# A recurrent block on one core: zero matmuls at the start, the identity on ScalarE's queue, halves in the first normalisation, another order of work

## The chip, the core and the metric

The kernel runs on one core of one Trainium2 chip. The core has five queues of work: TensorE (PE: matmuls, with the loads of their stationary operands listed apart as PEld), VectorE (DVE), ScalarE (ACT), GpSimd (POOL) and SyncE (SP, which here only issues DMAs). The metric is the device time of one execution in microseconds (us), the median over the runs. All arithmetic is in 32-bit floats.

## The reference

Eight sequences of 256 rows and 512 channels go through one block: a token-shifted mix of inputs, a recurrence over time for 32 heads of 16 channels, and a gated feed-forward part. Cut to what matters:

```python
xn = _ln(x, ln1_w, ln1_b)
sx = _token_shift(xn, state[:, i1])                 # previous row minus this row
xxx = tanh((xn + sx * maa_x) @ maa_w1)              # 5 groups of 32
xxx = matmul(xxx, maa_w2)
x5 = xn[:, :, None] + sx[:, :, None] * (maa_stack + xxx)
w = exp(-exp(time_decay + tanh(x5[:, :, 1] @ decay_w1) @ decay_w2))
r, k, v = x5[3] @ Wr.T, x5[0] @ Wk.T, x5[2] @ Wv.T
g = silu(x5[4] @ Wg.T)
def step(s, rkvw):                                  # 256 steps, per head a 16 x 16 state
    a = k_t[:, :, :, None] * v_t[:, :, None, :]
    out = einsum('bhk,bhkd->bhd', r_t, u * a + s)
    return (a + w_t[:, :, :, None] * s, out)
att = group_norm(outs) * gn_w + gn_b
x = x + att * g @ Wo.T
xn2 = _ln(x, ln2_w, ln2_b); sx2 = _token_shift(xn2, state[:, i0])
rr = sigmoid((xn2 + sx2 * ffn_maa_r) @ ffn_Wr.T)
kk = square(relu((xn2 + sx2 * ffn_maa_k) @ ffn_Wk.T))
x = x + rr * (kk @ ffn_Wv.T)
```

## The kernel before

The work of one sequence (a batch, b from 0 to 7) is cut into three stages, each written by one function: `inputs_of_scan` (first normalisation, mixing, the projections to k, v, r, g and the decay w), `scan` (the recurrence) and `rest` (group norm, output projection, second normalisation, feed-forward). In one phase the kernel works on the first stage of one batch, the second of the batch before and the third of the one before that.

Rows lie on partitions only for the normalisation; then PE turns them (`turned`, the transposes against the identity `idt`), and from there on channels lie on the 128 partitions, in four blocks, two to a tile ("q" counts the two halves of the channels). PE's results go to eight banks: six tiles `ps` of one bank each and the tile `wrep`, which holds the decays of a scan. ScalarE and VectorE read them out.

The recurrence runs on VectorE as a scan along time. For each block of 128 channels of k there are four scans of 1024 elements (`st<-wrep,vs`, line 885). Before each, v is written to memory (`vo`), read back repeated over partitions (`vs<-vo`, a DMA of 512 KB), its first column is filled by ScalarE (line 876) and it is multiplied by k (line 883, on DVE, or line 880 on POOL). After it, POOL multiplies by r (line 888), and PE sums over the state's rows with a matmul against a constant, which is called the gather here (line 896).

No scheduler of the language orders the work. The stage functions only add pieces of work (`plan.add`, with an engine, an estimated length, the buffers written and read) to a `Plan`. Its table `TURNS` holds one rank for each of the 2,643 pieces. `order` takes the ready piece of lowest rank, gives it a start from the estimates, takes its buffers from the pools, and finally sorts all pieces by start: that is the order in which each engine's queue is filled. The estimates are `LATENCY` (what passes from the end of a piece on one engine until another engine may use its result), `LANDS` (the same for DMAs), `SWITCH`, `AHEAD` and `GAP`. They only decide the order and which buffer a piece gets; on the chip every engine runs its queue in order and waits on semaphores.

The start concerns the prediction most. For batch 0 the normalisation is written differently (`alone`): VectorE takes the statistics of the two halves of the rows (lines 554 and 555), ScalarE the square root of both (line 557), VectorE the reciprocal (559) and the two scaled copies xh (562). PE turns them (588). With `first` given, the input of the first mixing matmul is built from xn times (1 - maa_x), to which the shifted rows times maa_x are added (622): before the change VectorE reads `ps` to make xn (595), and ScalarE reads the same `ps` to make the product (598), for which `owners` folds the norm's weights into the table `ow`. Then come the mixing matmul (401, with weights `mw`), a tanh on ScalarE (680), a matmul against `mw2a`, and the mixed inputs (703 to 720).

`mul` (line 396) writes all larger matmuls, with the stationary operand as one piece of 128 columns or as four of 32 that run beside each other, as the plan's `tiles` decides. In the profile one matmul of 32-bit floats is two records, a transpose is one.

Of the kernel before, what the change touches and what calls it, by code (L numbers as in the profile page):

```python
# [67 lines left out]
class Plan:  # L68
# [4 lines left out]
    LATENCY = {"PE": 0.12, "DVE": 0.09, "ACT": 0.09, "POOL": 0.09, "DMA": 1.65}  # L73
    LANDS = {"vs__": (2.3, 1.8), "rsb_": (0.9, 2.0), "sq_": (0.9, 2.0), "s": (0.2, 1.9), "vo_": (0.75, 2.2), "vo__": (0.38, 2.2), "o_": (0.75, 1.1), "x": (1.6, 1.7), "xt": (1.6, 1.7), "xs": (0.7, 0.9), "rd": (0.4, 1.4)}
# [40 lines left out]
    def stage(self):  # L115
# [225 lines left out]
def tile_rwkv_block(  # L341
# [73 lines left out]
    dw1, dw2 = const("dw1", [P, NK, DEC]), const("dw2", [2 * DEC, E])  # L415
    hm = const("hm", [P, NK, 32])
    eh = const("eh", [P, 4])
    ow = const("ow", [P, 2, NK])
    W = {n: [const(f"W{n}{h}", [P, 2, E]) for h in range(2)] for n in "kvrg"}

    pool("s0", 2, [P, NK, S])
# [50 lines left out]
    def load(buf, src, kb):  # L472
        dma(buf, lambda: src, buf, kb)
# [641 lines left out]
```

## Time and profile before

| | |
|---|---|
| median of 3 runs | 616.62 us (616.23 to 616.91) |
| the profiled execution | 616.02 us |
| its span, first to last instruction | 614.2 us |
| PE busy | 593.8 us (97%) |
| VectorE busy | 546.0 us (89%) |
| POOL busy | 522.3 us (85%) |
| ScalarE busy | 515.8 us (84%) |
| DMA | 124.73 MB, mean 203 GB/s |

All times in the views count from the start of the span. A row of the timeline gives start, length, engine, line, operation, output and inputs by the program's names, the tile's shape and how many instructions are merged, and in brackets the idle time before them and what ended it. A row of the busy time by stage gives the stretch, its length, the busy time of PE, weight loads, VectorE, ScalarE and POOL, the granted clock, the share of the DMA engines and GB/s. A row of the waits gives the total, the number and the longest.

### The profile page before, as it was taken

Reading aid. Unit: us, or ns where it says so; the run is one execution under the profiler, and the core shown is the slowest. Engines: PE = TensorE matmul, PEld = TensorE weight load, DVE = VectorE, ACT = ScalarE, POOL = GpSimd, SP = SyncE. Lnnn points to the kernel's source line nnn. Section 1 sums busy time; section 2 is a strip of 40 time slices with the busy share of each in tenths; the row PEclk is TensorE's granted clock in tenths of the full one; section 3 lists DMA queues with packets and bytes.
Section 4 is the critical chain, followed back from the end, with each engine's and each line's share of the span. In section 5 each row is a group of like instructions: output and inputs, shape, how many; then the busy total and the mean of one; then the engine's idle time right before and its main releaser. Section 6 shows DMA issues by size and latency. Waiting matters only on the chain.

```text
span 614.2 us, 17191 instructions
## 1 busy us (share of the span) xinstructions
PE 593.8 (97%) x7068; PEld 345.9 (56%) x7068; DVE 546.0 (89%) x487; ACT 515.8 (84%) x1171; POOL 522.3 (85%) x421
## 2 busy tenths in 40 slices
PE   4899999899999999999999999999999999999997
PEld 4575656457544764357653885465644474456463
DVE  5789999999999989799898999999999999995432
ACT  4878878999999989999999798999899799966431
POOL 2799999999989999899978999999969998897030
PEclk9999999999999999999999999999999999999999
DMA  8887779568969777867777896796958698681551
GB/s 291 272 199 184 194 186 257 141 176 211 273 174 255 188 187 211 212 201 208 221 188 221 269 230 181 179 273 166 246 142 221 174 257 233 203 238 36 195 186 46
DMA packets 52493, 124.73 MB, mean 203 GB/s; under 512 B 5824, under 2 KB 11200, under 8 KB 52416
## 3 DMA queue, kind: packets, MB, share of 16 engines
q1 hardware_dynamic: 48048, 119.46, 71.2%
q10 hardware_dynamic: 4368, 4.20, 2.2%
q8 instruction: 55, 0.90, 0.7%
q14 instruction: 22, 0.18, 0.1%
HBM read 115.25 MB, written 8.39 MB: 201 GB/s over the span
## 4 chain that ended last, share of the span: by engine, by line
PE 73%; ACT 13%; POOL 5%; DVE 4%; issue 2%; DMA 1%; ACTq 0%; SPq 0%; POOLq 0%; DVEq 0%
PE ps L401 61%; PE ps L896 8%; PE ps L588 2%; ACT att L846 1%; PE ps L760 1%; POOL st L888 1%; ACT wrep L866 1%; POOL mix L720 1%; ACT sq L951 1%; ACT rk L951 1%; DVE st L885 1%; DMA idt<-in_consts 1%; ACT vs L876 1%; ACT att L957 1%; ACT L866 1%
## 5 line engine op out<-in xcount | busy, mean ns | idle before, releaser
L885 DVE TENSOR_TENSOR_SCAN st<-wrep,vs 128x1024 f32<-128x1024 f32 x128 | 289.5, 2280 | 4.1 <-ACT wrep L866 1.0
L888 POOL TENSOR_TENSOR st<-st,r 128x1024 f32<-128x1024 f32 x128 | 254.4, 2001 | 6.2 <-DVE st L885 5.7
L883 DVE TENSOR_TENSOR vs<-vs,ps 128x1024 f32<-128x1024 f32 x122 | 144.2, 1207 | 2.4 <-ACT vs L876 2.1
L401 PE MATMUL ps<-Ws,mix 128*32 128x512 f32 (+1 forms) x864 | 115.0, 589 | 0.8 <-ACT o L986 0.8
L401 PEld LDWEIGHTS ps<-Ws,mix 128*32 128x32 f32 (+1 forms) x864 | 37.4, 116 | 64.8 <-issue 56.9
L720 POOL TENSOR_TENSOR mix<-mix,xn 128x512 f32<-128x512 f32 x62 | 66.7, 1090 | 7.6 <-DVE mix L705 7.6
L896 PE MATMUL ps<-st,con 128*32 128x256 f32 x1024 | 61.6, 380 | 0.9 <-POOL st L888 0.4
L401 PE MATMUL ps<-mix,Wv 128*32 128x256 f32 (+1 forms) x748 | 60.0, 380 | 0.3 <-DVE mix L717 0.3
L401 PE MATMUL ps<-mix,Wr 128*32 128x256 f32 (+1 forms) x616 | 59.2, 380 | 0.6 <-ACT vs L876 0.6
L401 PE MATMUL ps<-mix,Wk 128*32 128x256 f32 (+1 forms) x856 | 58.5, 380 | 0.5 <-DVE x L968 0.3
L401 PE MATMUL ps<-mix,Wg 128*32 128x256 f32 (+1 forms) x712 | 58.6, 379 | 0.0
L401 PE MATMUL ps<-mix,Ws 128*32 128x256 f32 (+1 forms) x688 | 58.0, 380 | 0.0
L401 PE MATMUL ps<-Ws,g 128*32 128x512 f32 (+1 forms) x416 | 56.6, 593 | 0.3 <-POOL g L962 0.2
L610 POOL TENSOR_TENSOR sx<-xn 128x512 f32<-128x512 f32 x31 | 32.3, 1052 | 27.5 <-ACT xn L605 22.5
L635 POOL TENSOR_TENSOR mix<-mix,xn 128x512 f32<-128x512 f32 x44 | 47.6, 1098 | 5.0 <-ACT mix L633 3.8
L846 ACT COPY att<-ps 32x256 f32<-32x256 f32 x128 | 46.7, 365 | 4.4 <-PE ps L838 2.3
L703 ACT ACTIVATE ps<-ps,vec 128x256 f32<-128x256 f32 x112 | 46.8, 443 | 4.1 <-PE ps L401 2.7
L401 PEld LDWEIGHTS ps<-mix,Wv 128*32 128x32 f32 (+1 forms) x748 | 40.2, 120 | 16.9 <-issue 2.3
L401 PEld LDWEIGHTS ps<-mix,Wr 128*32 128x32 f32 (+1 forms) x616 | 40.6, 128 | 16.1 <-POOL mix L720 1.1
L401 PEld LDWEIGHTS ps<-mix,Ws 128*32 128x32 f32 (+1 forms) x688 | 39.9, 123 | 16.1 <-ACT mix L633 0.8
L896 PEld LDWEIGHTS ps<-st,con 128*32 128x32 f32 x1024 | 32.5, 110 | 28.0 <-POOL st L888 4.7
L401 PEld LDWEIGHTS ps<-mix,Wg 128*32 128x32 f32 (+1 forms) x712 | 39.0, 122 | 15.6 <-issue 0.3
(133 smaller groups left out, 968.0 us busy)
## 6 DMA issues: line engine op xcount, KB each, us to landing
vs<-vo SPq DMA_DIRECT2D x128, 512.0 KB, 5.5
Ws<-in_wo SPq DMA_DIRECT2D x16, 512.0 KB, 5.3
Ws<-in_fr SPq DMA_DIRECT2D x16, 512.0 KB, 6.3
Ws<-in_fk SPq DMA_DIRECT2D x16, 512.0 KB, 7.2
Ws<-in_fv SPq DMA_DIRECT2D x16, 512.0 KB, 4.9
x<-in_x SPq DMA_DIRECT2D x9, 512.0 KB, 6.5
vo<-v ACTq DMA_DIRECT2D x15, 256.0 KB, 4.6
out<-o SPq DMA_DIRECT2D x15, 256.0 KB, 4.4
```

The costliest lines, as they stand in the source:

```text
L401: nc.tensor.matmul(out[i : i + n], lhsT=w[:, i : i + n], rhs=x, start=first, stop=final)
L588: nc.tensor.transpose(ps()[:, m, n * P : (n + 1) * P], xh[n]()[:, k * P : (k + 1) * P], idt())
L610: take(512, [sx], [xn], lambda xn=xn, sx=sx, e=nc.vector if quick else nc.gpsimd: e.tensor_tensor(sx(), xn()[:, :, 0:T], xn()[:, :, 1 : T ...
L635: gp(512, t, [t, xn[q]], lambda q=q, t=t: nc.gpsimd.tensor_tensor(t(), t(), xn[q]()[:, :, 1 : T + 1], ALU.add))
L703: act(256, p_, [p_, vec], lambda g=g, q=q, m=m, p_=p_: nc.scalar.activation(p_()[:, m, :], p_()[:, m, :], AF.Identity, bias=col(f"maa_{g}" ...
L720: gp(512, t, [t, xn[q]], lambda q=q, t=t: nc.gpsimd.tensor_tensor(t(), t(), xn[q]()[:, :, 1 : T + 1], ALU.add))
L846: act(350, atts[q], [pc], lambda i=32 * (2 * q + m), m=m, q=q, h=32 * h: nc.scalar.copy(atts[q]()[h : h + 32, m, :], pc()[i : i + 32, 0, :]))
L866: act(4 * T, w, [ew], lambda m=m, w=w, ew=ew: nc.scalar.activation(w()[:, :, 1:T], ew()[:, m : m + 1, 0 : T - 1].to_broadcast([P, 4, T - 1 ...
L883: dve(4 * T, [vs], [vs, kp], lambda m=m, vs=vs, kp=kp: nc.vector.tensor_tensor(vs(), vs(), kp()[:, m : m + 1, :].to_broadcast([P, 4, T]), ...
L885: dve(4 * T, [st], [w, vs], lambda w=w, vs=vs, st=st: nc.vector.tensor_tensor_scan(st().rearrange("p n t -> p (n t)"), w().rearrange("p n ...
L888: gp(4 * T, st, [st, r], lambda m=m, st=st, r=r: nc.gpsimd.tensor_tensor(st(), st(), r()[:, m : m + 1, :].to_broadcast([P, 4, T]), ALU.mul ...
L896: nc.tensor.matmul(pat()[32 * i : 32 * i + 32, 0, :], lhsT=con()[:, s : s + 32], rhs=done[i]()[:, j, :], start=(j == 0), stop=(j == 3),)
```

## The change

Six edits:

1. `LATENCY` grows: PE from 0.12 to 0.24 us, DVE and ACT from 0.09 to 0.14, POOL from 0.09 to 0.10; `LANDS` gets an entry for `idt`. `TURNS` is replaced by another table of ranks, for 2,643 pieces of work again (the other edits add three and remove three).
2. `warmed`: seven matmuls of 128 x 256 zeros, into a `ps` tile that nothing reads; the zeros are written by a memset on VectorE at the start.
3. The identity is loaded by a DMA that ScalarE issues, instead of the fourth DMA of SP's queue.
4. For batch 0's first normalisation, each half of the rows has its own statistics, square root, reciprocal and scaled copy.
5. For batch 0, ScalarE makes the product from xn (in SBUF) instead of from `ps`.
6. `owners` becomes one instruction, 1 - maa_x.

```diff
-    LATENCY = {"PE": 0.12, "DVE": 0.09, "ACT": 0.09, "POOL": 0.09, "DMA": 1.65}
+    LATENCY = {"PE": 0.24, "DVE": 0.14, "ACT": 0.14, "POOL": 0.1, "DMA": 1.65}
...
     TURNS = """
-        5 50 8 34 35 59 43 77 41 122 129 94 125 138 20 21 22 23 145 146 152 153 18 2 26 19 38 57 32 39 58 31 33 56 44 60
...
-    ow = const("ow", [P, 2, NK])
+    ow = const("ow", [P, NK])
...
+    warm = plan.pools["xn"][3][1]
+    nc.vector.memset(warm[:, 0, :], 0.0)
...
+    def warmed():
+        ps = new("ps", "psa")
+
+        def mm():
+            for n in range(7):
+                nc.tensor.matmul(ps()[:, 0, :], lhsT=warm[:, 0, 0:P], rhs=warm[:, 0, 0:T], start=True, stop=True)
+
+        pe(5.3, [ps], [], mm)
+
     def owners():
-        i, j = (VECS.index(v) for v in ("maa_x", "ln1_w"))
-        for n in range(2):
-            gp(4, ow, [vec], lambda n=n: nc.gpsimd.tensor_tensor(
-                ow()[:, n, :], vec()[:, :, j + n], vec()[:, :, i], ALU.mult), 30)
-        for n in range(2):
-            gp(4, ow, [vec, ow], lambda n=n: nc.gpsimd.tensor_tensor(
-                ow()[:, n, :], vec()[:, :, j + n], ow()[:, n, :], ALU.subtract), 30)
+        i = VECS.index("maa_x")
+        gp(4, ow, [vec], lambda: nc.gpsimd.tensor_scalar(ow(), vec()[:, :, i], -1.0, 1.0, ALU.mult, ALU.add), 30)
...
+            if first:
+                for n in range(NT):
+                    t, s, st = new("xh", f"xh{u}_{n}"), src[n], new("st", f"st{u}_{n}")
+                    mv, rs = (mv, rs) if n == 0 else (new("mv", f"mv{u}_{n}"), new("rs", f"rs{u}_{n}"))
+                    dve(512, [st], [s], lambda st=st, s=s: nc.vector.bn_stats(out=st(), in_=s()))
+                    dve(6, [mv], [st], lambda n=n, st=st, mv=mv: nc.vector.bn_aggr(out=mv()[:, n, :], in_=st()), 8)
+                    act(1, rs, [mv, eh], lambda n=n, mv=mv, rs=rs: nc.scalar.activation(
+                        rs()[:, n : n + 1], mv()[:, n, 1:2], AF.Sqrt, bias=eh()[:, 0:1]), "sqrt", 1)
+                    dve(1, [rs], [rs], lambda n=n, rs=rs: nc.vector.reciprocal(rs()[:, n : n + 1], rs()[:, n : n + 1]), 6.25)
+                    dve(512, [t], [s, mv, rs], lambda n=n, t=t, s=s, mv=mv, rs=rs: nc.vector.tensor_scalar(
+                        t(), s(), mv()[:, n, 0:1], rs()[:, n : n + 1], ALU.subtract, ALU.mult), 0.55)
+                    xh.append(t)
+                return turned(xh, which, row, b, alone, first)
...
-                    act(256, t, [ps, ow], lambda m=m, k=k, t=t, ps=ps: nc.scalar.activation(
-                        t()[:, m, :], ps()[:, m, :], AF.Identity,
-                        bias=ow()[:, 1, k : k + 1], scale=ow()[:, 0, k : k + 1]), pointers=2)
+                    act(256, t, [xn, ow], lambda m=m, k=k, t=t, xn=xn: nc.scalar.activation(
+                        t()[:, m, :], xn()[:, m, 1 : T + 1], AF.Copy, scale=ow()[:, k : k + 1]), pointers=1)
...
-    load(idt, consts[:, 0:P], 64)
+    plan.add("ACT", 0.4, [idt], [], lambda: nc.scalar.dma_start(out=idt(), in_=consts[:, 0:P]), kb=64)
...
+    warmed()
     owners()
```

More of the change, by code (lines that the diff above doesn't have):

```diff
@@ L68 @@
 class Plan:
-    LATENCY = {"PE": 0.12, "DVE": 0.09, "ACT": 0.09, "POOL": 0.09, "DMA": 1.65}
-    LANDS = {"vs__": (2.3, 1.8), "rsb_": (0.9, 2.0), "sq_": (0.9, 2.0), "s": (0.2, 1.9), "vo_": (0.75, 2.2), "vo__": (0.38, 2.2), "o_": (0.75, 1.1), "x": (1.6, 1.7), "xt": (1.6, 1.7), "xs": (0.7, 0.9), "rd": (0.4, 1.4)}
+    LATENCY = {"PE": 0.24, "DVE": 0.14, "ACT": 0.14, "POOL": 0.1, "DMA": 1.65}
+    LANDS = {"vs__": (2.3, 1.8), "rsb_": (0.9, 2.0), "sq_": (0.9, 2.0), "s": (0.2, 1.9), "vo_": (0.75, 2.2), "vo__": (0.38, 2.2), "o_": (0.75, 1.1), "x": (1.6, 1.7), "xt": (1.6, 1.7), "xs": (0.7, 0.9), "idt": (0.2, 2.2), "rd": (0.4, 1.4)}
     SWITCH = {"ACT": 1.3, "PE": 0.12}
@@ L538, in normed @@
             mn, nm = new("mn", f"mn{u}"), new("nm", f"nm{u}")
-        if (which == 1 and b > 1) or (which == 2 and b < 5):
+        if (which == 1 and b > (1)) or (which == 2 and b < 5):
             junk = [new("xh", f"xh{u}_{n}") for n in range(NT)]
```

238 rows, old and new, of the table TURNS are left out of this document.

## The prediction

> **What bounds the kernel now.** I read the busy time by stage first.
>
> ```profile
> 0.00:7.25 7.25, 0.00 (x1) 0.03 (x1) 2.80 (x8) 1.78 (x3) 0.50 (x12) 1.00 0.66 213
> 7.25:16.11 8.86, 8.35 (x49) 7.36 (x49) 5.96 (x12) 5.61 (x12) 3.31 (x8) 1.00 1.05 363
> 16.11:26.59 10.48, 8.94 (x101) 5.84 (x101) 9.15 (x19) 9.02 (x25) 8.00 (x8) 1.00 0.78 283
> 26.59:60.00 33.41, 32.52 (x436) 21.42 (x440) 29.27 (x27) 27.89 (x66) 32.34 (x28) 1.00 0.82 202
> 60.00:120.00 60.00, 57.35 (x1012) 35.01 (x1008) 58.55 (x47) 50.37 (x110) 59.68 (x40) 1.00 0.74 188
> ...
> 200.00:260.00 60.00, 58.23 (x729) 32.67 (x725) 54.01 (x45) 56.45 (x130) 53.93 (x45) 1.00 0.75 201
> 260.00:580.00 320.00, 319.73 (x3709) 183.48 (x3702) 295.79 (x245) 280.47 (x631) 281.52 (x221) 1.00 0.74 204
> 580.00:614.20 34.20, 29.26 (x97) 17.06 (x95) 11.56 (x23) 8.12 (x16) 5.58 (x5) 1.00 0.37 123
> ```
>
> The columns after the length are PE, weight loads, DVE, ACT and POOL. From 260 to 580 us TensorE is idle for 0.27 us of 320: nothing can be won there, only lost. All that can be won is idle time of PE elsewhere: 7.25 us before its first matmul, 0.51 and 1.54 us in the two stages after it, 0.89, 2.65 and 1.77 us in the next stages shown, and 4.94 us in the last. From 60 to 120 us DVE (58.55) and POOL (59.68) are as full as PE, so a gain at the start survives only if all three start earlier. The waits of PE, longest first, say who ends this idle time:
>
> ```profile
> PE ps L588 <- DMA idt<-in_consts: 7.2, 1, 7.2
> PE ps L401 <- ACT v L791: 1.3, 1, 1.3
> PE ps L401 <- ACT o L986: 1.2, 2, 0.8
> ```
>
> **The head.** The timeline of the first 16 us:
>
> ```profile
> 2.10 0.47 SPq L390 DMA_DIRECT2D idt<-in_consts  x1
> ...
> 3.33 1.36 DVE L554 BATCH_NORM_STATS2 st<-xt 128x6 f32<-128x512 f32 x2 [2.48 <-DMA xt<-in_x]
> 4.61 0.30 DVE L555 BATCH_NORM_AGGREGATE mv<-st 128x2 f32<-128x6 f32 x2
> ...
> 5.27 0.17 DVE L559 RECIPROCAL rs<-rs 128x2 f32<-128x2 f32 x1 [0.36 <-ACT rs L557]
> 5.47 1.00 DVE L562 TENSOR_SCALAR xh<-xt,mv,rs 128x512 f32<-128x512 f32 x2
> 5.51 0.53 SPq L390 DMA_DIRECT2D mw2a<-in_maa_w  x1
> ...
> 7.25 1.94 PE L588 MATMUL ps<-idt,xh 128*128 128x128 f32 x8 [7.25 <-DMA idt<-in_consts]
> ...
> 8.44 0.56 ACT L598 ACTIVATE mix<-ps,ow 128x256 f32<-128x256 f32 x1 [0.92 <-PE ps L588]
> ...
> 9.04 1.45 DVE L595 TENSOR_SCALAR xn<-ps,vec 128x256 f32<-128x256 f32 x3 [2.57 <-ACT mix L598]
> ...
> 10.07 1.48 ACT L598 ACTIVATE mix<-ps,ow 128x256 f32<-128x256 f32 x3 [0.98 <-DVE xn L595]
> ...
> 14.23 0.65 DVE L622 SCALAR_TENSOR_TENSOR mix<-xn,vec,mix 128x256 f32<-128x256 f32 x1
> ...
> 15.67 0.39 ACT L680 ACTIVATE ta<-ps 128x256 f32<-128x256 f32 x1 [1.11 <-PE ps L401]
> ...
> 16.11 1.15 PE L401 MATMUL ps<-ta,mw2a 32*128 32x256 f32 x16
> ```
>
> *Identity by ScalarE's queue.* The normalised rows xh are ready at 5.47 + 1.00 = 6.47, but the transposes start at 7.25, when the identity has landed; it was issued at 2.10, fourth on SP. Issued first on ScalarE's queue, before its table load, it leaves at about 0.7 and is no longer last: the transposes can start at about 6.5, **-0.75 us**. Its 64 KB now run beside the two halves of x; at the 213 GB/s of the first row that is 0.3 us at worst for the second half, and DVE needs that half 0.7 us after the first: +0.1 us. ScalarE's table load behind the issue slips by the length of an issue, under 0.5 us by these rows, and the square root that follows it waits for DVE's statistics anyway.
>
> *Halves.* On DVE the path from 3.33 to 6.47 takes 3.14 us. In halves DVE does two statistics (1.36), two aggregates (0.30), two reciprocals (2 x 0.17) and two subtractions (1.00), 3.0 us with no wait for ScalarE in the middle (the square root of one half lies beside the other half's work) but with more steps that depend on the one before. I take **0**, with 0.3 either way.
>
> *Seven zeros.* They cost PE time only before 6.5 us, when it has nothing else. What they buy is the clock:
>
> ```profile
> 9.00:10.00 1.00, 1.00 (x5) 1.00 (x6) 1.00 1.02 356
> 11.30:12.30 1.00, 1.00 (x12) 1.00 (x11) 1.00 1.07 371
> ...
> 583.97 1.09 PE L588 MATMUL ps<-idt,xh 128*128 128x128 f32 x8 [0.40 <-DVE xh L562]
> ```
>
> The same 128-column matmuls go from 5 to 12 in a microsecond (first two rows, the count behind PE), so the clock rose between 2.75 and 4.05 us after PE began at 7.25, though the clock column says 1.00 in both; and the eight transposes that take 1.94 us at the start take 1.09 us at 584 us. Half of the difference lies before ScalarE's and VectorE's first read of the result: **-0.45 us**. The zeros wait for a memset on DVE and begin near 1.2 us; each is two records of 256 columns, and with 0.20 to 0.24 us for 128 cold columns (one of five in a microsecond; 1.94 / 8) I take 0.43 us for one. If the clock rises 3.4 us after their start, eight of the fourteen are cold, six take half, and they end at 1.2 + 3.4 + 1.3 = 5.9 us, before xh; if all stay cold, at 1.2 + 14 x 0.43 = 7.2 us.
>
> *Two readers of one bank.* In the rows above ScalarE and VectorE take turns: each of the first reads from ps ends the other's idle time (DVE idle 2.57 us behind ACT, ACT 0.98 us behind DVE). The change lets VectorE alone read ps, and ScalarE read the xn that VectorE wrote. On VectorE's queue xn was normalised in pieces with its products between them, and a statistic of the next batch before the last product (both cut from the order of instructions; xn_99 and xn_100 are the halves of the channels, mix_107 and mix_108 the sums):
>
> ```order
> L595 TENSOR_SCALAR xn_99<-ps_170,vec 128x256 x2
> L595 TENSOR_SCALAR xn_100<-ps_171,vec 128x256
> L622 SCALAR_TENSOR_TENSOR mix_107<-xn_99,vec,mix_107 128x256
> L595 TENSOR_SCALAR xn_100<-ps_171,vec 128x256
> L622 SCALAR_TENSOR_TENSOR mix_107<-xn_99,vec,mix_107 128x256
> L622 SCALAR_TENSOR_TENSOR mix_108<-xn_100,vec,mix_108 128x256
> L554 BN_STATS st_90<-x_161 128x6
> L622 SCALAR_TENSOR_TENSOR mix_108<-xn_100,vec,mix_108 128x256
> ```
>
> Now:
>
> ```order
> L613 TENSOR_SCALAR xn_99<-ps_170,vec 128x256
> L613 TENSOR_SCALAR xn_100<-ps_171,vec 128x256
> L613 TENSOR_SCALAR xn_99<-ps_170,vec 128x256
> L613 TENSOR_SCALAR xn_100<-ps_171,vec 128x256
> L639 SCALAR_TENSOR_TENSOR mix_107<-xn_99,vec,mix_107 128x256 x2
> L639 SCALAR_TENSOR_TENSOR mix_108<-xn_100,vec,mix_108 128x256 x2
> L572 BN_STATS st_90<-x_161 128x6
> ```
>
> The statistics went behind the products, and nothing in the block waits in turns.
>
> ```profile
> L622 DVE SCALAR_TENSOR_TENSOR mix<-xn,vec,mix 128x256 f32<-128x256 f32 x4 | 2.8, 718 | 0.0
> ...
> L595 DVE TENSOR_SCALAR xn<-ps,vec 128x256 f32<-128x256 f32 x4 | 2.0, 540 | 3.3 <-ACT mix L598 3.3
> ```
>
> From 8.44 to the last product's end, 14.23 + 0.65 = 14.88, it took 6.44 us; four xn (2.0) and four products (2.8) with 0.1 us for the hand-over are 4.9: **-1.5 us**, up to -2.4 if the products take the 0.47 us of the shortest. ScalarE's own path (its four products a step behind xn, two copies, a table load before the tanh) is as long, so I take -1.7, not the far end.
>
> The tanh thus starts -0.75 + 0.1 - 0.45 - 1.7 = **-2.8 us** earlier. What needs it next is the matmul at 16.11, which also needs mw2a:
>
> ```profile
> mw2a<-in_maa_w SPq DMA_DIRECT2D x1, 256.0 KB, 6.9
> ```
>
> Issued at 5.51, it landed at 12.4. The same bytes stand ahead of it now, so no more than 16.11 - 12.4 = 3.7 us can be won here. Behind the tanh POOL's chain sets the pace to 26.59:
>
> ```profile
> 18.15 0.80 ACT L572 ACTIVATE xh<-x,nm,rs 128x512 f32<-128x512 f32 x1
> 18.85 0.46 ACT L709 ACTIVATE mix<-ps,vec 128x256 f32<-128x256 f32 x1
> ...
> 19.39 2.96 POOL L711 TENSOR_TENSOR mix<-mix,sx 128x512 f32<-128x512 f32 x2 [2.35 <-ACT mix L709]
> ```
>
> ScalarE put this 0.80 us row of the next batch between the two L709 copies; in the new order both stand together ahead of it: up to -0.8 for POOL, of which I take -0.4, since POOL's second multiply now waits for copies behind those rows. **Head: -3.2 us**, from -1.2 (late clock, no gain on ScalarE) to -3.8.
>
> **The middle.** One of the long waits has a place that can be followed. It is where PE starts the last mixing matmul (mw2b) of the third batch:
>
> ```profile
> 115.28 1.91 PE L401 MATMUL ps<-mix,Wk 128*32 128x256 f32 x32
> 118.50 0.71 PE L401 MATMUL ps<-tb,mw2b 32*128 32x256 f32 x8 [1.31 <-ACT v L791]
> ```
>
> PE's queue there before (ps_172 is the product with Wv, which ScalarE has still to copy out):
>
> ```order
> L401 MATMUL ps_172<-mix_114,Wv_76 32x256 x8
> L401 MATMUL ps_172<-mix_111,Wv_77 32x256 x8
> L401 MATMUL ps_173<-mix_116,Wk_74 32x256 x8
> L401 MATMUL ps_173<-mix_109,Wk_75 32x256 x8
> L401 MATMUL ps_172<-tb_122,mw2b 128x256
> ```
>
> and now (ps_171 is the product with Wk):
>
> ```order
> L400 MATMUL ps_171<-mix_120,Wk_74 32x256 x8
> L400 MATMUL ps_171<-mix_109,Wk_75 32x256 x8
> L400 MATMUL ps_170<-mix_113,Wr_78 32x256 x8
> L400 MATMUL ps_170<-mix_117,Wr_79 32x256 x8
> L400 MATMUL ps_170<-mix_113,Wr_78 32x256 x8
> L400 MATMUL ps_170<-mix_117,Wr_79 32x256 x8
> L400 MATMUL ps_173<-tb_122,mw2b 128x256
> L400 MATMUL ps_171<-tb_122,mw2b 128x256
> ```
>
> Between the last product in a bank and its reuse lay half a projection (the 1.91 us of the first row); now a whole one lies there, and the 1.31 us fit into it: -1.3. The gather behind it reuses ps_170 at once, where PE must wait for that bank's copy as it did here for its own, with a shorter product between; I give back 0.4, a third of the wait: **-0.9 us**, between -1.3 and 0. The other waits between 26.59 and 260 us I leave as they are, with 2 us either way: the order moves nearly every row there, and no row of this trace prices the new ones.
>
> **The tail.**
>
> ```profile
> 602.61 1.28 ACT L986 ACT_TABLE_LOAD   x1 [5.64 <-PE ps L401]
> 603.90 1.08 ACT L986 ACTIVATE o<-ps 128x512 f32<-128x512 f32 x2
> 605.04 5.44 PE L401 MATMUL ps<-Ws,mix 128*128 128x256 f32 x20 [0.78 <-ACT o L986]
> ```
>
> PE waits 0.78 us for ScalarE to empty the bank that the last matmuls reuse, and ScalarE first loads a table. The last rows of PE's queue before (ps_170 and ps_172 hold the gate's products, mix_116 and mix_109 the squares):
>
> ```order
> L401 MATMUL ps_172<-Ws_165,mix_110 128x512 x2
> L401 MATMUL ps_171<-Ws_166,mix_116 128x512 x2
> L401 MATMUL ps_170<-Ws_166,mix_116 128x256 x2
> L401 MATMUL ps_170<-Ws_167,mix_109 128x256 x2
> L401 MATMUL ps_171<-Ws_167,mix_109 128x512 x2
> ```
>
> and now (ps_171 and ps_174 hold the gate, mix_108 and mix_115 the squares):
>
> ```order
> L400 MATMUL ps_174<-Ws_165,mix_113 128x512 x2
> L400 MATMUL ps_175<-Ws_166,mix_108 128x512 x2
> L400 MATMUL ps_175<-Ws_167,mix_115 128x512 x2
> L400 MATMUL ps_171<-Ws_166,mix_108 128x256 x2
> L400 MATMUL ps_171<-Ws_167,mix_115 128x256 x2
> ```
>
> Four wide matmuls now stand between the gate and the first reuse of its bank, where two stood. The 5.44 us of the row are two wide and eight narrow ones, twelve units of 256 columns, 0.45 us each, so two more wide ones cover 1.8 us, and the sigmoid's table is in from the batch before: **-0.8 us**. What follows the last matmul (605.04 + 5.44 to 614.2) stays.
>
> **Sum.** The profiled execution took 616.0 us (614.2 of span and 1.8 around it): 616.0 - 3.2 - 0.9 - 0.8 = 611.1. The median of the runs lies 0.6 above that execution, so **611.7 us**; alone this case reaches from 609.3 to 613.8.
>
> **Rivals.** *The loads of v set the pace* (613.0). For it:
>
> ```profile
> 22.84 0.35 ACTq L810 DMA_DIRECT2D vo<-v  x1
> ...
> 39.88 0.30 ACT L876 ACTIVATE vs<-s,cm 128x4 f32<-128x4 f32 x1 [0.28 <-DMA vs<-vo]
> ```
>
> v leaves just as the bulk of the weights has landed; three microseconds earlier it would share the queues with them, and at 39.88 one vs was already waited for. Then only 2 us of the head survive. Against it: this is the only such wait at the start of the scan, and it is short.
>
> *The clock rises late* (612.9). The zeros end at 7.2 instead of 6, after xh, and the transposes are still slow: 0.7 + 0.45 us of the head are lost. The Trainium skill ("TensorE: Matmul & The Clock Gate", What's actually happening) says that the window in which activity is judged runs free, about 3.4 us long, so the rise can fall anywhere up to a window later; the one rise this trace holds does not contradict it.
>
> *The head's gain is lost on the way* (616): POOL and DVE are full from 60 to 120 us, and if they start no earlier, PE only waits longer there. Against it: POOL's first long chain starts at 19.39 behind ScalarE, which is itself earlier.
>
> *Slower* (618.6): the longer ways in the table hold ps banks longer, and the new order makes PE wait for a copy out of a bank between 260 and 580 us, where it waits for nothing now. One such wait costs 1.31 us (118.50); from 6.2 / 1.31, five of them, the gain and 1.2 us more are gone, and six or seven more over six batches give 618 to 619. Against it: the planner now counts 0.24 us behind PE where it counted 0.12.
>
> **How the numbers follow.** Forecast 0.58, loads of v 0.13, late clock 0.08, lost on the way 0.08, slower 0.09, more than forecast 0.04 (a second long wait gone, 609). Below 0.2% (1.2 us) nothing can be told from no change here. Faster: the forecast, the two cases at 613 and the better one, 0.83; same 0.07; slower 0.10. The range, 609.0 to 615.6, holds the first three cases and part of the fourth.
>
> **What would show it.** Transposes at about 6.5 us in about 1.1 us; tanh near 12.9; PE's wait for the identity gone, none for ScalarE near 115 and 602 us; PE's idle time between 26.59 and 260 us at or under 6. It is wrong if PE idles more than 2 us between 257 and 577, or if ScalarE's waits for vs at the start of the scan grow past 1 us.

## The result, and the profile after

| | before | after |
|---|---|---|
| median of 5 runs beside each other | 616.62 us (615.34 to 617.93) | 613.26 us (611.67 to 613.54) |
| the profiled execution | 616.02 us | 613.54 us |
| its span | 614.2 us | 611.7 us |

The two medians lie 3.4 us apart; the ratio over all these runs is 0.9937, with an interval from 0.9915 to 0.9959. The prediction was 611.7, with a range from 609.0 to 615.6. The five runs of the changed kernel form two groups: 611.67 and 611.86 us with a mean granted clock of 1.0 (1.0 is PE's full speed), and 613.26, 613.39 and 613.54 with 0.997. The profiled execution is one of the second group. Here and below, medians leave out executions that were slow over their whole length: one of 3549 us (the kernel with the head undone), and two of 633 us with a mean clock of 0.949 (the kernel before with three of the head's edits), of which one is that kernel's only profile. PE's busy time by the same stages as before, first the head:

```profile
0.00:7.25 7.25, 5.46 (x20) 4.36 (x21) 3.09 (x11) 2.25 (x6) 0.69 (x13) 1.00 0.74 201
7.25:16.11 8.86, 8.40 (x76) 6.97 (x74) 7.69 (x15) 6.99 (x14) 3.89 (x6) 1.00 1.06 372
16.11:26.59 10.48, 9.09 (x104) 6.44 (x108) 6.26 (x14) 6.36 (x18) 9.56 (x10) 0.84 0.78 283
26.59:60.00 33.41, 32.30 (x436) 21.83 (x432) 29.99 (x30) 28.29 (x70) 30.48 (x25) 1.00 0.88 203
60.00:120.00 60.00, 58.92 (x1010) 39.12 (x1002) 58.93 (x49) 50.66 (x112) 59.98 (x41) 1.00 0.75 195
...
260.00:580.00 320.00, 319.04 (x3920) 179.58 (x3913) 294.36 (x245) 276.93 (x622) 280.52 (x219) 1.00 0.73 200
```

The clock column of the third row is new: 0.84. PE's waits, longest first:

```profile
PE ps L400 <- DVE mix L734: 1.8, 1, 1.8
PE ps L523 <- DVE xn L461: 1.2, 1, 1.2
PE ps L400 <- DVE mix L722: 1.1, 3, 0.6
PE ps L400 <- DVE o L1026: 1.0, 2, 0.8
PE ps L777 <- POOL mix L737: 0.6, 1, 0.6
```

The 7.2 us for the identity are gone, and the 1.3 for v and the 1.2 for o. A wait of 1.8 us for VectorE's addition L734 is new and now the longest. The timeline of the head shows where it lies:

```profile
1.17 4.75 PE L523 MATMUL ps<-xn 128*128 128x256 f32 x14 [1.17 <-DVE xn L461]
6.54 1.09 PE L606 MATMUL ps<-idt,xh 128*128 128x128 f32 x8 [0.62 <-DVE xh L566]
9.05 3.23 DVE L639 SCALAR_TENSOR_TENSOR mix<-xn,vec,mix 128x256 f32<-128x256 f32 x4
13.11 0.38 ACT L697 ACTIVATE ta<-ps 128x256 f32<-128x256 f32 x1
15.63 1.27 POOL L728 TENSOR_TENSOR mix<-mix,sx 128x512 f32<-128x512 f32 x1 [0.47 <-ACT mix L726]
15.78 1.66 DVE L734 TENSOR_TENSOR mix<-mix,xn 128x512 f32<-128x512 f32 x1
17.50 1.80 PE L400 MATMUL ps<-mix,Wv 128*128 128x256 f32 x4 [1.76 <-DVE mix L734]
19.09 1.91 PE L606 MATMUL ps<-idt,xh 128*128 128x128 f32 x8
```

Up to the tanh all went as forecast: transposes at 6.54 in 1.09 us, the tanh at 13.11 (12.9 forecast, 15.67 before). Then PE waits 1.76 us, and the next eight transposes, at 19.09, take 1.91 us again. The busy time of shorter stretches tells why:

```profile
4.15:17.81 13.66, 11.18 (x89) 9.19 (x89) 11.66 (x25) 9.41 (x22) 5.71 (x8) 1.00 1.04 347
17.81:21.22 3.41, 3.41 (x13) 2.94 (x12) 3.33 (x10) 1.02 (x2) 3.33 (x4) 0.50 1.05 385
21.22:26.59 5.37, 5.37 (x92) 3.20 (x94) 1.23 (x4) 3.69 (x11) 4.61 (x7) 1.00 0.51 182
```

From 17.81 to 21.22 the granted clock is 0.50, half of full speed. To see what became of the head's gain I use the gathers (L896 before, L913 after). The ones below have the same amount of matmul work ahead of them on PE in both orders (but for the zeros; some of it is cut into other shapes), so the difference of two starts is time won or lost up to there. A row gives the shortest, median and longest of 32 matmuls in ns, then when the first and the last of them start. Before, and then after:

```profile
L896 PE MATMUL ps<-st,con x32: 379/379/403, 55.6 to 57.2; 128*32 128x256 f32 x32
L896 PE MATMUL ps<-st,con x32: 379/379/403, 222.5 to 224.1; 128*32 128x256 f32 x32
L896 PE MATMUL ps<-st,con x32: 379/379/379, 249.9 to 251.4; 128*32 128x256 f32 x32
L896 PE MATMUL ps<-st,con x32: 379/379/403, 436.8 to 438.4; 128*32 128x256 f32 x32
L896 PE MATMUL ps<-st,con x32: 379/379/379, 472.6 to 474.1; 128*32 128x256 f32 x32
L896 PE MATMUL ps<-st,con x32: 379/379/403, 561.0 to 562.6; 128*32 128x256 f32 x32
```

```profile
L913 PE MATMUL ps<-st,con x32: 379/379/379, 54.6 to 56.1; 128*32 128x256 f32 x32
L913 PE MATMUL ps<-st,con x32: 379/379/403, 221.5 to 223.0; 128*32 128x256 f32 x32
L913 PE MATMUL ps<-st,con x32: 379/379/379, 247.7 to 249.3; 128*32 128x256 f32 x32
L913 PE MATMUL ps<-st,con x32: 379/379/403, 434.6 to 436.1; 128*32 128x256 f32 x32
L913 PE MATMUL ps<-st,con x32: 379/379/379, 471.1 to 472.7; 128*32 128x256 f32 x32
L913 PE MATMUL ps<-st,con x32: 379/379/403, 559.7 to 561.2; 128*32 128x256 f32 x32
```

To the hundredth, by the traces, the differences are -1.08, -1.07, -2.12, -2.24, -1.49 and -1.37 us, and -2.51 at the end of the span. So the head gave 1.1, the stretch to 222 us nothing, 222 to 250 gave 1.1, 250 to 437 another 0.1, 437 to 473 took 0.7 back and the rest up to 561 another 0.1, and the tail gave 1.1. Over the two long stretches, of 167 and 187 us, the difference moves by 0.01 and 0.12 us: what PE has won by then stays.

### The profile page after: what moved, and what is told of

It reads as the page before. It is cut to its first block, busy times and chain, and to the rows that moved or that the text cites. A ratio compares the mean times of both kernels' runs of the same rounds, so it can differ in the third digit from the quotient of the medians.

```text
span 611.7 us, 17692 instructions
## 1 busy us (share of the span) xinstructions
PE 599.6 (98%) x7322; PEld 350.8 (57%) x7322; DVE 545.4 (89%) x489; ACT 514.3 (84%) x1172; POOL 522.3 (85%) x418
## 4 chain that ended last, share of the span: by engine, by line
PE 84%; ACT 5%; DVE 5%; POOL 3%; issue 1%; DMA 0%; ACTq 0%; DVEq 0%; POOLq 0%
PE ps L400 70%; PE ps L913 8%; PE ps L606 2%; PE ps L777 2%; POOL st L905 1%; ACT ps L720 1%; DVE st L902 1%; ACT rk L968 1%; ACT sq L968 1%; POOL g L979 1%; PE ps L855 1%; PE ps L939 0%; DMA xt<-in_x 0%; DVE mix L639 0%; DVE mix L722 0%
## 5 line engine op out<-in xcount | busy, mean ns | idle before, releaser
L400 PE MATMUL ps<-Ws,mix 128*32 128x512 f32 (+2 forms) x864 | 115.4, 589 | 0.2 <-DVE o L1026 0.2
L737 POOL TENSOR_TENSOR mix<-mix,xn 128x512 f32<-128x512 f32 x62 | 67.0, 1098 | 5.5 <-DVE mix L722 5.3
L400 PE MATMUL ps<-mix,Wv 128*32 128x256 f32 (+1 forms) x808 | 61.6, 381 | 1.8 <-DVE mix L734 1.8
L913 PE MATMUL ps<-st,con 128*32 128x256 f32 x1024 | 62.3, 380 | 0.1
L400 PE MATMUL ps<-mix,Wk 128*32 128x256 f32 (+1 forms) x904 | 60.0, 379 | 0.6 <-DVE mix L722 0.6
L400 PEld LDWEIGHTS ps<-mix,Wk 128*32 128x32 f32 (+1 forms) x904 | 39.0, 113 | 18.1 <-issue 1.5
L913 PEld LDWEIGHTS ps<-st,con 128*32 128x32 f32 x1024 | 32.7, 110 | 27.6 <-issue 5.5
```

The costliest lines, as they stand in the source:

```text
L400: nc.tensor.matmul(out[i : i + n], lhsT=w[:, i : i + n], rhs=x, start=first, stop=final)
L737: gp(512, t, [t, xn[q]], lambda q=q, t=t: nc.gpsimd.tensor_tensor(t(), t(), xn[q]()[:, :, 1 : T + 1], ALU.add))
L913: nc.tensor.matmul(pat()[32 * i : 32 * i + 32, 0, :], lhsT=con()[:, s : s + 32], rhs=done[i]()[:, j, :], start=(j == 0), stop=(j == 3),)
```

## The experiments

Medians are of 5 to 12 runs, with those of the kernel before taken beside them (615.95 to 616.16 us). "At full clock" means a mean granted clock of 0.999 or 1.0.

**Filling PE's wait.** Four matmuls into the bank that the product restarts:

```
                     def mm(m=m, ps=ps, ks=ks):
+                        for n in range(4 if m == 0 and ks == turns[0] else 0):
+                            nc.tensor.matmul(ps()[:, m, :], lhsT=idt(), rhs=w2a()[:, 0:T], start=True, stop=True)
```

> Four matmuls of 256 columns (identity times mw2a, into the bank that the product with Wv starts anew) stand on PE where it idles 1.76 us, from 15.7 to 17.5 us, behind VectorE's addition. Theory (the clock was halved for 3.41 us from 17.81 on because PE had idled, and only in some runs of the changed kernel): no stretch at half clock after 10 us, mean clock 1.0 in all runs, transposes near 19 us in 1.1 instead of 1.9 us, all runs near 611.7, median 1.5 lower than 613.3. Rival (the half clock comes from something else, and the two groups of runs with it): both groups stay, at 611.8 and 613.4. Rival (the fillers delay the real product): 17.50 becomes 17.7 or later and nothing is won.

Measured: 612.36 us (611.74 to 613.00), ratio 0.9939 (0.9925 to 0.9953), all five runs at full clock. Its timeline:

```profile
15.93 1.99 PE L823 MATMUL ps<-mw2a,idt 128*128 128x256 f32 x8
17.76 1.03 PE L400 MATMUL ps<-mix,Wv 128*128 128x256 f32 x4
18.62 1.04 PE L606 MATMUL ps<-idt,xh 128*128 128x128 f32 x8
```

The half clock is gone, and the transposes take 1.04 us. But the median is 0.9, not 1.5 lower than 613.3: these runs spread over 1.3 us by themselves, at full clock, and what spreads them was not settled. The fillers held the product up by little: it starts 0.18 us behind the end of VectorE's addition (17.58), against 0.06 in the changed kernel.

**No zeros.** `for n in range(7)` in `warmed` became `range(0)`.

> The changed kernel without the seven matmuls of zeros; everything else, the order too, is the same. The prediction's term: the eight transposes take 1.9 instead of 1.1 us and the tanh starts 0.45 us later (13.6 instead of 13.11), so 0.45 us more: 612.2 in runs without the later half clock, 613.8 in those with it. Rival (the gain is lost behind POOL's and VectorE's work): tanh later, time the same within 0.2. Rival (the zeros also set whether the clock is halved at 17.8, by where its windows fall): the shares of the two groups change, and the median moves by up to 1.6 either way.

Measured: 614.04 us (613.19 to 615.74), ratio 0.9967 (0.9957 to 0.9977); nine runs at full clock, 613.2 to 614.2, and three at 0.997, 615.2 to 615.7. The profiled one, by stretches:

```profile
5.93:9.34 3.41, 2.73 (x13) 2.73 (x14) 1.86 (x5) 0.68 (x3) 0.00 (x0) 1.00 1.00 332
...
16.16:19.58 3.42, 1.66 (x16) 1.11 (x9) 3.35 (x6) 2.59 (x7) 2.89 (x3) 1.00 1.05 390
19.58:22.99 3.41, 3.41 (x17) 2.57 (x19) 3.37 (x10) 1.04 (x3) 3.33 (x3) 0.50 1.02 367
```

PE begins at 6.61; the clock record of the trace rises at 9.34, and the transposes take 1.97 us. From their start to the end of the last product it takes 6.60 us instead of 5.74: the 0.86 between is the whole difference of the transposes, where the forecast took half of it. The tanh starts at 14.10 instead of 13.11, so the zeros are worth about twice the forecast 0.45. The last two rows are again a window of 3.41 us, half of it idle, and a halved one behind it.

**The product from ps again, in the new order.**

```
-                    act(256, t, [xn, ow], ... t()[:, m, :], xn()[:, m, 1 : T + 1], AF.Copy, scale=ow()[:, k : k + 1]) ...
+                    act(256, t, [xn, ow], ... t()[:, m, :], ps()[:, m, :], AF.Identity,
+                        bias=ow()[:, 1, k : k + 1], scale=ow()[:, 0, k : k + 1]) ...
```

> ScalarE's four products of the first batch read the bank ps again, as in the kernel before, instead of xn, in the changed kernel's order. The prediction's term (two readers of one bank take turns, 1.7 us): from the first xn at 7.24 to the last product 1.5 to 1.7 us longer, tanh near 14.7, time up by about 1.5. Rival (what cost the time was the order on VectorE, pieces with products and a statistic between): tanh within 0.4 us of 13.11 and time up by no more than 0.4.

Measured: 613.31 us (612.16 to 613.91), ratio 0.9950 (0.9937 to 0.9964). On VectorE:

```profile
7.32 1.00 DVE L621 TENSOR_SCALAR xn<-ps,vec 128x256 f32<-128x256 f32 x2 [0.75 <-PE ps L614]
8.57 1.00 DVE L621 TENSOR_SCALAR xn<-ps,vec 128x256 f32<-128x256 f32 x2 [0.25 <-ACT mix L624]
9.48 3.23 DVE L648 SCALAR_TENSOR_TENSOR mix<-xn,vec,mix 128x256 f32<-128x256 f32 x4
```

For this run `ow` holds both columns again. One turn of 0.25 us is left of the alternation; the transposes started at 6.63, so the path takes 6.08 us, 0.34 more than 5.74, and the tanh comes at 13.54, 0.43 later than 13.11. In the new order the second reader is cheap. The median can't price so little, since both groups of runs are in it. Two kernels further down price the reader in the old order.

**POOL quiet beside L734.** The two POOL operations of that tile emit nothing in the first batch.

> Left out: POOL's multiplication and addition for one tile of the mixed input of the decay (group 1, channels 256 to 511) in the first batch, which ran at 15.63 and 16.97 us beside VectorE's addition at 15.78. Theory (VectorE's addition of two tiles of SBUF took 1.66 us because POOL worked on tiles of SBUF beside it; 0.68 us is what it takes alone): it takes about 0.7 us, PE's wait behind it falls from 1.76 to about 0.8 us and the clock stays at 1.0. Rival (it waited for something of its own, such as the xn of the tile): 1.4 us or more still. The time is 1 to 3 us lower; part of that is the work left out on POOL.

Measured: 611.31 us, one run, at full clock.

```profile
16.43 0.69 DVE L735 TENSOR_TENSOR mix<-mix,xn 128x512 f32<-128x512 f32 x1
...
18.41 1.36 POOL L728 TENSOR_TENSOR mix<-mix,sx 128x512 f32<-128x512 f32 x1 [2.60 <-ACT mix L726]
```

With POOL idle the addition takes 0.69 us, and PE's wait falls to 0.79. (It begins later than 15.78, as the head does here: the clock of this execution rose only at 7.16, the zeros lasted until 7.41, and the transposes began at 7.24.) That settles what made it long. In the changed kernel POOL's L728 began 0.15 us ahead of it and ended at 16.90; the addition ended at 17.44, 0.54 later, as if it had stood still until POOL was done. The Trainium skill ("SBUF — State Buffer", Who interferes with whom) says that a VectorE instruction with two inputs in SBUF contends with a GpSimd instruction that reads SBUF, over a pair of ports that the two share under an exclusive lock; these rows agree.

**The head undone in the new order; three of its edits in the old order.** The first has the identity on SyncE's queue behind the first weights, no zeros, and the product from ps. The second is the kernel before in its own order, but that each of ScalarE's products goes behind the xn it now reads:

```
+    nc.scalar.dma_start(out=idt(), in_=consts[:, 0:P])
     nc.scalar.activation(plan.pools["mn"][1][1], eh()[:, 0:2], AF.Sqrt)
...
     with tc.manual_schedule():
+        for n in range(7):
+            nc.tensor.matmul(
+                plan.pools["ps"][5][1][:, 0, :], lhsT=warm[:, 0, 0:P], rhs=warm[:, 0, 0:T], start=True, stop=True)
```

and the product from xn, with `ow` as in the change.

> The changed kernel with the head's edits undone in its own order: identity on SyncE's queue again behind both halves of x, the vectors and the first weights, no zeros, ScalarE's products read ps. What is left of the change is the new turns and the statistics in halves. Theory formed from the runs so far (the order on VectorE and ScalarE gave most of the head's gain that the prediction put on the two readers of a bank): the transposes at 7.2 in 1.9 us, the tanh near 14.5 (15.67 before), the time 1.5 to 2 us below the kernel before, near 614.3. Rival (the prediction's terms): the tanh at 15.6 to 15.9, the time only 1.7 below by the middle and the tail. Rival (the order gives nothing): within 0.5 of before.

> The kernel before, its order on every engine kept, with three of the head's edits: identity first on ScalarE's queue, seven matmuls of zeros, ScalarE's products of the first batch from xn. Not in it: the halves and the new turns. Theory (order): transposes at 6.5 in 1.1 us, tanh 1.2 to 1.8 us earlier than 15.67, near 14.2, since VectorE's queue still has pieces of xn, products and a statistic in turn; the time 1.2 to 1.8 below before, PE's waits of the middle and the tail as before. Rival (prediction's term, two readers of a bank): tanh near 12.9, time 2.8 below.

Measured: 615.05 us (613.92 to 616.37), ratio 0.9986 (0.9977 to 0.9995), with the head undone; four of its eleven runs are at 0.997. 613.88 us, ratio 0.9973 (0.9963 to 0.9983), with the old order; all seven at full clock. So the turns and the halves alone give about 1 us, and these three edits about 2: that is between the theory's 1.2 to 1.8 and the rival's 2.8. The theory for the first kernel fell: the tanh came at 15.98, not at 14.5, near the rival's 15.6 to 15.9. PE, without zeros, ran at half clock until 12.66 by the clock record of its trace, and the matmuls with the centred weights, which it runs ahead of the tanh's input, lasted for 5.07 us (3.42 in the changed kernel):

```profile
8.93 5.07 PE L400 MATMUL ps<-Ws,Ws 128*128 128x128 f32 x28
```

Its first rows on VectorE price the halves:

```profile
3.38 0.69 DVE L569 BATCH_NORM_STATS2 st<-xt 128x6 f32<-128x512 f32 x1 [2.20 <-DMA xt<-in_x]
...
5.65 0.55 DVE L574 TENSOR_SCALAR xh<-xt,mv,rs 128x512 f32<-128x512 f32 x1
```

xh is ready 2.82 us after the first half landed, against 3.14 before: the halves win 0.32. And x lands earlier than the 3.68 of the changed kernel, where the identity ran beside it: that costs about 0.3. In the second kernel 5.75 us pass from the transposes at 7.14 to the end of the last product, as in the changed kernel. This is a hint only, from the profile named above; the medians do not need it.

**The same with the product from ps** prices the two readers in the old order.

> The kernel before, its order on every engine kept, with the identity first on ScalarE's queue and seven matmuls of zeros; ScalarE's products read ps as before. Beside the run that had the products from xn too, it prices the two readers of one bank in the old order, with a warm PE. From the start of the transposes to the end of the last product it took 7.63 us before and 5.75 us in that run. The prediction's term (1.5 to 1.7 us by two readers and pieces in turn): about 7.3 us here, time 615.3. Theory from the runs so far (PE at half clock took half of it, the bank the rest): 6.7 us, time 614.8. Rival (nearly all of it was the clock): 6.1 us, time 614.2.

Measured: 615.31 us (615.00 to 616.63), ratio 0.9993 (0.9984 to 1.0001). So the identity and the zeros alone give some 0.6 us in the old order, within the noise of nothing, where the forecast had 1.1 for them. The transposes start at 6.97 instead of 7.25, held up by x, which landed 0.36 later (3.69 instead of 3.33), and from there to the last product it takes 7.13 us instead of 7.63. For the two readers the prediction's term was nearly right here: 1.4 us lie between this median and 613.88, and the timeline shows the alternation with a warm PE:

```profile
6.97 1.04 PE L591 MATMUL ps<-idt,xh 128*128 128x128 f32 x8
...
8.27 1.45 DVE L598 TENSOR_SCALAR xn<-ps,vec 128x256 f32<-128x256 f32 x3 [1.44 <-ACT mix L601]
...
10.81 0.55 DVE L598 TENSOR_SCALAR xn<-ps,vec 128x256 f32<-128x256 f32 x1 [0.70 <-ACT mix L601]
...
13.45 0.65 DVE L625 SCALAR_TENSOR_TENSOR mix<-xn,vec,mix 128x256 f32<-128x256 f32 x1
```

From 6.97 to 14.10 are 7.13 us, 1.38 more than with the product from xn. The order and the product's source each remove most of the same alternation: 6.08 us with the new order alone, 5.75 (the hint above) with the new source alone, 5.74 with both.

**The changed kernel again.**

> The changed kernel once more. Theory (the clock is judged on windows of 3.41 us, which lie anew in each run; the 1.76 us of PE's wait halves it only if one window holds nearly all of it): about half the runs show the lower mean clock and lie 1.6 us above the others, 611.7 against 613.4. Rival (it belongs to one chip or one day): one group only.

Measured: 612.68 us (611.98 to 614.24), ratio 0.9948 (0.9936 to 0.9959): three runs at full clock (611.98 to 612.68), two at 0.997 (613.27, 614.24). Both groups are there. Its profiled execution is at full clock throughout, though PE waited the same 1.76 us, from 16.08 to 17.84. Its clock rose at 4.00, so a window of 3.413 us ended at 17.66, inside the wait, and no window held more than 1.58 us of it. Its first and last gathers:

```profile
L913 PE MATMUL ps<-st,con x32: 379/379/379, 53.2 to 54.8; 128*32 128x256 f32 x32
...
L913 PE MATMUL ps<-st,con x32: 379/379/403, 558.2 to 559.7; 128*32 128x256 f32 x32
```

Against before these are -2.4 and -2.8, and the span is 610.2, -4.0. The half clock cost the other execution 1.4 to 1.5 us, at the first gather as at the last.

**The tail's piece moved back.**

```
+        at = [n for n, op in enumerate(done) if op.engine == "PE" and op.bufs[0].name in ("psfv7_0", "psfv7_1_0")]
+        done.insert(at[1], done.pop(at[2]))
```

> The changed kernel with one piece moved back: the second half of the last wide product with fv goes behind the first narrow one, as in the kernel before. The prediction's term: PE waits 0.78 us near 602 us for ScalarE's o again, and the time is 0.8 us above the changed kernel. Rival (o comes earlier now for another reason, and the piece does not matter): no wait, the same time.

Measured: 612.89 us (612.82 to 614.37), ratio 0.9958 (0.9946 to 0.9971).

```profile
605.32 1.99 PE L400 MATMUL ps<-Ws,mix 128*128 128x256 f32 x8 [0.85 <-DVE o L1026]
```

The wait is back with 0.85 us, now put down to VectorE's reader of the bank. The gather of 561 us lies 3.15 ahead of before and the end of the span 3.2: the tail's gain of 1.1 is gone with this one piece. The medians, 612.89 and 612.68, mix runs with and without the half clock and don't show it; of the runs at full clock alone, the middle one of four is near 612.86 here, and that of the changed kernel's five is 611.98.

**Versions without the wait.** In the first, the bank adds xn and the tile, and VectorE's addition goes behind the other tile's:

```
+                        direct = m == 0 and ks == turns[0]
+                        for k in ks if direct else ():
+                            mul(ps()[:, m, :], vs_[k]()[:, m * P : (m + 1) * P], xn[1]()[:, k % 2, 1 : T + 1], k == begin, False)
```

> The changed kernel; the first half of the first product with Wv (PE at 17.50, after 1.76 us of waiting for VectorE's addition of xn) now adds in the bank: two matmuls with xn and two with the tile not yet added to, and VectorE's addition goes behind that of the other tile. Nothing is left out. Theory: four matmuls of 0.43 us from 15.75 to 17.5 take the place of 1.76 us of waiting and two matmuls, so everything behind comes 0.8 us earlier, and the clock is not halved in any run: 610.9 in a run with an early clock, median 611.3. Rival (VectorE's addition of the other tile, now ahead, or the next mixing tiles become late): PE waits again at 19 to 22 us, and it is no faster than 611.8.

Measured: 611.86 us (611.35 to 613.05), ratio 0.9934 (0.9922 to 0.9946), all at full clock. That misses the theory's 611.3 and fits the rival's "no faster than 611.8": PE waits again, 0.31 us at 20.32. The second sends the identity by SyncE's queue, fourth, ahead of the first weights:

> The version with the sum in the bank (two matmuls with xn in the place of PE's wait at 16 to 17.5 us), and the identity fourth on SyncE's queue, behind both halves of x and the vectors and ahead of the first weights, instead of first on ScalarE's. Theory (the identity's 64 KB beside x made x land 0.35 us later, 3.1 instead of 2.7 us after its issue; here it lands behind x but well before 6.2 us): xh at 6.2 instead of 6.55, transposes at 6.2, the time 0.3 below that version, 611.4 by the median. Rival (the identity lands after 6.2, since it stands behind x on one queue): transposes at 6.5 or later, no gain or a loss of up to 0.7.

Measured: 611.87 us (611.27 to 612.35), ratio 0.9934 (0.9920 to 0.9947). x came earlier, but nothing was won:

```profile
1.17 6.09 PE L523 MATMUL ps<-xn 128*128 128x256 f32 x14 [1.17 <-DVE xn L461]
7.10 1.04 PE L606 MATMUL ps<-idt,xh 128*128 128x128 f32 x8
```

xh was ready at 6.29. In this run the clock rose at 6.88, so the zeros lasted until 7.26 and held the transposes up. The third has six zeros:

> The version before with six matmuls of zeros instead of seven. There x came earlier and xh was ready at 6.29, but the transposes started at 7.10, since the clock rose only at 6.88 and the zeros, at half clock till then, ended at 7.26. Twelve records of 0.43 us from 1.17 on end at 6.3 at the latest. Theory (the rise comes with the end of a window of 3.41 us, about 4 to 7 us from the start, and with seven zeros about four runs in ten delay the transposes by up to 0.8 us): transposes at 6.3 to 6.4 whenever the clock rises, median 611.5, the slowest run under 612.3. Rival (six are too few, the clock rises a window later in some runs): a run above 612.8, with transposes of 1.9 us if it is the profiled one.

Measured: 611.57 us (611.25 to 612.59), ratio 0.9928 (0.9914 to 0.9942) to a before of 616.16.

```profile
6.45 1.34 PE L606 MATMUL ps<-idt,xh 128*128 128x128 f32 x8
```

The clock rose even later here (7.07), and the transposes still began at 6.45. One run was slower (612.59) than the theory allowed, so a late rise under the zeros is not all that spreads the runs at full clock. This version has the lowest median, some 1.1 us below the changed kernel's 612.68, but the two intervals overlap.

## Why the prediction came out as it did

| step of the sum | forecast | measured |
|---|---|---|
| identity, with x beside it | -0.65 | -0.3 alone in the old order (7.25 to 6.97, x 0.36 later); -0.7 with the halves (7.25 to 6.54) |
| halves | 0 | -0.3 |
| zeros | -0.45 | -0.5 in the old order (7.63 to 7.13), -0.9 in the new one (6.60 to 5.74); 1.4 by the medians 614.04 and 612.68 |
| two readers of one bank | -1.7 | -1.4 in the old order, -0.3 in the new one |
| tanh | -2.8 | -2.6 |
| head in all | -3.2 | -2.4 at full clock, -1.1 with the half clock |
| middle, near 118 us | -0.9 | 0 up to 222 us |
| middle, elsewhere | 0 | -1.1 from 222 to 250, +0.7 from 437 to 473 |
| tail | -0.8 | -1.1 |

**The head** was right up to the tanh, and nearly so by terms. Counted from the kernel before, a warm PE gave 0.5 us (0.45 forecast), and the product's source with the order another 1.39 (7.13 to 5.74; 1.7 forecast). The two edits are not simply added: once the alternation is gone, leaving out the zeros costs 0.86.

**The step that failed**, though the time came out within the range, is the one behind the tanh: "Behind the tanh POOL's chain sets the pace to 26.59", with another 0.4 to win. POOL's first multiplication did come 3.76 us earlier (19.39 to 15.63), but VectorE's addition for the first product with Wv set the pace there, and POOL now worked beside it. The new turns had also put that product ahead of the next batch's transposes on PE. Before:

```
MATMUL ps_175<-ta_121,mw2a 128x256
MATMUL ps_172<-idt,xh_88 128x128
...
MATMUL ps_171<-idt,xh_87 128x128
MATMUL ps_170<-mix_111,Wv_77 128x256 x2
```

and now:

```
MATMUL ps_175<-ta_121,mw2a 128x256
MATMUL ps_172<-mix_111,Wv_77 128x256 x2
MATMUL ps_171<-idt,xh_88 128x128
```

So one wait of 1.76 us stands where two shorter ones had been, and it is just long enough to halve the clock in some runs. The prediction read the order at this place for ScalarE's rows only. Of the 1.6 us between 611.7 and the median of 613.26, this half clock is nearly all: the two runs without it took 611.67 and 611.86. That these meet the forecast so closely is partly luck. Counted alike, by the profiled execution at full clock, the forecast was 611.1 and 611.98 was measured, 0.9 less of a gain; the 0.6 that was added for the median hides that.

**The middle.** PE's wait for ScalarE's v went, as forecast, yet from the gather at 56 us to that at 222 nothing was won. PE's idle time there fell from 3.2 to 1.5 us, but its busy time grew by as much. Part of that can be placed, at the mixing matmul itself:

```profile
116.91 1.40 PE L400 MATMUL ps<-tb,mw2b 32*128 32x256 f32 x8 [0.43 <-DVE vs L900]
```

Its four matmuls (eight records) took 0.71 us before, side by side. Now the first begins at 116.91, and the other three only at 117.60, when ScalarE's copy of k out of ps_171 (L808, which ends at 117.56) frees that bank. This wait of 0.69 us for a bank counts as busy time in the merged row, and with the 0.43 ahead of it 1.1 of the old 1.31 us are back. So the step "the 1.31 us fit into it" failed: a whole projection was not enough. Another new wait is 0.64 us for POOL's L737 at 101.67. The other 1.0 us by which PE's busy time grew is not placed.

What was won instead, 222 to 250 us, was not forecast. Two waits that the prediction had left alone, 0.30 us for ScalarE's squares at 228.66 and 0.42 for its o at 245.33, stand in the trace of before and not after; the other 0.3 of the 1.1 is not placed. The 0.7 lost from 437 to 473 go with two new stops, 0.47 at 450.51 (nothing the profile names) and 0.20 at 460.77; what lies behind the first was not tried. Up to that loss the middle gave 1.2 us, near the 0.9 forecast, but by other waits at another place: that is luck.

**The tail** was the mechanism forecast. The wide matmuls now run on into the narrow ones without a wait:

```profile
594.07 13.92 PE L400 MATMUL ps<-Ws,mix 128*128 128x512 f32 x40
```

Undone, the piece gave back 0.85 us as a wait and the whole 1.1 in the end.

**The rivals.** The loads of v: no wait of ScalarE for vs at the start of the scan. Late clock: it does occur, but the one execution whose transposes it held up and whose other work was whole, at 7.10 instead of 6.3, took 611.78 us, under the median of its kernel; whether it spreads the runs at full clock is not shown. Head lost on the way: no, the gathers carry it unchanged to 222 us. New waits between 260 and 580: PE idles 0.96 us there instead of 0.27, so 0.7 more, not 6.

## What to carry to other kernels

When a reordering takes slack out ahead of a point, ask what the next instruction on the bound engine will wait for and which engines will work beside that one: here an addition of two SBUF tiles met POOL, and cost 1 us. Idle time of PE that is near half of a clock window can cost twice, first itself and then the half clock behind it, as in 15 of 43 runs here, so a wait that can't be removed is worth filling. Useful matmuls that take work off another engine did so at 611.86 us, plain fillers at 612.36, with intervals that overlap. In a kernel bound by PE, compare the starts of instructions with the same work ahead of them in both orders; that tells in a few rows where time was won and lost, which busy shares don't.

## What the runs showed of the hardware

- The clock is judged in windows of 3.41 us that lie anew in each run. In the traces every stretch between two changes of the granted clock is a multiple of 3.413 us (13.65 = 4, 604.16 = 177), but the first rise came 2.73 to 5.99 us after PE's first matmul. Late rises, the prediction's rival, do occur: at 6.88, 7.07 and 7.16, which is 0.6 to 0.9 us after the first batch's rows were ready (6.29, 6.17 and 6.51).
- PE idle for 1.76 us, 52% of a window, was enough to halve it: in 15 of 43 runs of the kernels that have this wait, and in none of the 20 of the four that filled or removed it, nor in the 18 in the old order. If the whole wait must lie in one window, (3.41 - 1.76) / 3.41 = 48% would be expected, where 35% were seen. One execution (the product from ps, its wait ending at 17.92) had 1.75 us in one window and kept its clock, so here the limit lies close to half. The Trainium skill ("TensorE: Matmul & The Clock Gate", What's actually happening) has the half clock come after at least one idle window of about 3.4 us; these traces show it with half a window.
- VectorE's addition of two SBUF tiles of 512 columns takes 0.69 us alone and 1.66 beside a POOL multiplication that began 0.15 us earlier.
- 64 KB on another queue, beside the two first pieces of x, of 256 KB each, made these land 3.0 to 3.3 us after their issue, instead of 2.7 to 2.8 in the four kernels that send the 64 KB behind them.
